# A planned GNN kernel: transfers planned by their size with late landings, PSUM banks held whole in the plan, one bank for each graph at the end, and the weight product cut where the loads of w_ih are cut

## The chip, the core and the metric

The kernel runs on one core of a Trainium2 chip. The metric is the device time of one execution in microseconds. The profile names the engines PE (matrix multiply), PEld (its weight loads), DVE (vector), ACT (scalar, activations), POOL (GpSimd) and SP, whose queue issues all DMAs here. Data is worked on in SBUF; matrix products land in PSUM, which has eight banks of 128 partitions x 512 fp32 columns.

## The reference

128 graphs of 128 nodes with 256 features each. Two blocks, each with a layer norm, a ReLU and a residual sum.

```python
def _L0_gnn_ref(x, adj, weight, w_ih, w_hh, b_ih, b_hh):
    A = (adj != 0).astype(x.dtype)
    h = x
    for i in range(3):
        m = jnp.einsum('bnd,de->bne', h, weight[i])
        aggr = jnp.einsum('bst,bsd->btd', A, m)
        h = _gru_cell(aggr, h, w_ih, w_hh, b_ih, b_hh)
    return h

def _L1_gnn_ref(h, adj, W):
    Wh = jnp.einsum('bnf,fo->bno', h, W)
    s = Wh.sum(axis=-1)
    e = jax.nn.leaky_relu(s[:, :, None] + s[:, None, :], negative_slope=ALPHA)
    e = jnp.where(adj == 0, -jnp.inf, e)
    alpha = jax.nn.softmax(e, axis=-1)
    return jnp.einsum('bpq,bqo->bpo', alpha, Wh)

h = jnp.maximum(_layernorm(x, axis=-1), 0.0)
x = x + _L0_gnn_ref(h, adj, L0_gnn_weight, L0_gnn_w_ih, L0_gnn_w_hh, L0_gnn_b_ih, L0_gnn_b_hh)
h = jnp.maximum(_layernorm(x, axis=-1), 0.0)
x = x + _L1_gnn_ref(h, adj, L1_gnn_W)
```

The GRU cell takes the products `inp @ w_ih.T` and `h @ w_hh.T` (three gates of 256 each), two sigmoids and one tanh.

## The kernel before

**Tiling.** Graphs are taken in 32 groups of four (`G = 4`). A group passes three GRU layers and then the attention. The message weight of a layer is multiplied into `w_ih` once at the start (`compose`, L622), so that a layer needs the edge sums of `h` and then products with two weight sets, `s_hh` (from `w_hh`) and `s_x0`, `s_x1`, `s_x2` (composed). Each product of two 256 x 256 blocks uses seven block products instead of eight: `node_sums` (L850) makes the sums `hs` and `gs` of blocks of data, `block_sums` (L534) those of the weights. Layers 0 and 1 keep features on the partitions (`product`, L887), layer 2 keeps nodes on the partitions (`product_rows`, L901). Several groups are in flight at a time; the list `turns` (L1091) fixes the order of their layers on PE.

**The planner.** Nothing in the loop over groups (L1429) emits an instruction. Each call of `op` (L94) records a node: engine, assumed duration in ns, a function that emits the instructions, and the tiles it reads and writes, from which the dependencies follow. `Plan.run` then orders the nodes and emits them, engine by engine, in that order. Each engine executes its own list in order; an instruction that has to wait holds back all that stand behind it on its engine. The order comes from a list schedule in assumed time (`go`, L247) that is tried many times with shaken priorities (`search`, L212), and the try with the least PE idle time plus a share of a measure of risk is kept. In the first 20 us and the last 120 us of PE work `EDGES` tries are made for each piece of the order, elsewhere `TRIES`.

**What the plan takes a DMA for.** An SP node costs its issue time (`kb * KB` ns in `load`, L500, 480 ns for the later loads) and then a fixed `lag` of 3600 ns (other numbers are given at single calls) until its data is there. If another DMA landed just before, it is taken to land at least `BEHIND` = 1200 ns after that one, whatever its size (L324). `x1` (L1131) and the rows of a later group (L1112) are 512 KB each and are often issued one right after the other. The first reader of the rows is DVE, `bn_stats` (L686) in `normed`.

**What the plan takes a PSUM bank for.** The program itself keeps two engines out of one bank: a bank is one tile. The plan before knows that a new user of a bank waits for the old one, but within one use it compares column ranges: where PE writes half 1 and DVE reads half 0, it takes both to run at the same time.

**The start.** `weights` (L553) loads the weights (two loads for the halves of `w_ih`, L571), transposes them through PSUM (`turned`, L511), composes and makes the block sums. The composed weight of 768 columns is made for each k in pieces of 512 and 256 columns (L619); both halves of `w_ih` must have been transposed for any piece. PSUM tiles are copied out by `to_sbuf` (L529).

**The end.** The third last group's and the second last group's attention ends with a product for each graph (L1286) and an addition into `x1` (L1295); two graphs share a bank, in its two halves. The last group works graph by graph: `weighed` (L1368) turns two graphs in one bank `p_h` (L1379), copies them out (L1382), multiplies them into one bank `p_w` (L1388) and copies that out (L1391); `by_graph` (L1395) has one bank `p_e` for the turned weights (L1404, copied out at L1406) and one bank `p_o` for the products (L1408), which L1411 adds into `x1`; L1414 writes each graph to DRAM. The scores are made in bank `x_n` (L1187, L1193, L1226), the maximum at L1235, the bound `low` at L1230 to L1233, the exponentials at L1250.

## Time and profile before

| what | us |
|---|---|
| median of three runs (2084.32 to 2087.18) | 2086.25 |
| the profiled execution, its own time | 2087.59 |
| its span in the profile | 2085.5 |
| DVE, ACT, POOL busy (share of the span) | 1688.3 (81%), 1619.1 (78%), 910.0 (44%) |

The profiled execution took 2.1 us more than its span, which is what lies before the first and after the last recorded instruction. The granted PE clock is 0.9 or more of full speed in all forty slices of the page. The span less PE's busy time is 16.3 us, and it lies like this:

| stretch of the span (us) | PE idle (us) |
|---|---|
| 0 to 30 | 4.10 |
| 30 to 200 | 0.59 |
| 200 to 1800 | 3.08 |
| 1800 to 2060 | 0.46 |
| 2060 to 2080 | 3.94 |
| 2080 to 2085.5 | 4.10 |

Issued DMAs of 512 KB landed after a median of 5.1 us (rows of a group) and 4.3 us (`x1`), those of 256 KB after 2.8 us, the transposing ones after 3.2 to 3.3 us. A duration of a matmul in the profile holds some 0.16 us in which the next one already runs: two fp32 passes with 256 columns take 0.59 us when they stand alone in a row, and the next row starts 0.43 us after them.

### The profile page before, as it was taken

To read this page: it belongs to the slowest core of one execution; us is meant where nothing else is said; L and a number is where in the kernel's file an instruction comes from. 1 tells how busy PE (TensorE), PEld (TensorE's weight loads), DVE (VectorE), ACT (ScalarE), POOL (GpSimd) and SP (SyncE) were. 2 spreads that over 40 slices of the span, in tenths; PEclk is the share of its full clock that TensorE was granted. 3 is DMA by queue.
4 is the path that set the end of the run, shared out by engine and by line. 5 is a ranking of instruction groups with operands and counts; after the bars stand their busy time and mean duration, and the time that the engine had idled before them with its cause. 6 is when DMAs were issued, how large, how long until landed. Compare 5 with 4: busy or idle time off the path is not lost.

```text
span 2085.5 us, 31660 instructions
## 1 busy us (share of the span) xinstructions
PE 2069.2 (99%) x10926; PEld 1660.3 (80%) x10926; DVE 1688.3 (81%) x3912; ACT 1619.1 (78%) x3007; POOL 910.0 (44%) x885
## 2 busy tenths in 40 slices
PE   9999999999999999999999999999999999999998
PEld 7887887778877778877788877788777888788875
DVE  6777887888878888887888887888888877788677
ACT  6677887788877788877888777878777886878775
POOL 4644544435434435444354434454443544445330
PEclk9999999999999999999999999999999999999999
DMA  5322233332333323233222333232333223323321
GB/s 147 66 64 43 56 69 72 73 69 43 69 74 71 76 47 71 61 79 73 65 49 66 82 66 76 49 64 66 76 76 61 46 67 77 61 44 67 64 66 36
DMA packets 369376, 138.12 MB, mean 66 GB/s; under 512 B 300608, under 2 KB 368960, under 8 KB 369216
## 3 DMA queue, kind: packets, MB, share of 16 engines
q1 hardware_dynamic: 369216, 136.10, 29.6%
q8 instruction: 86, 1.41, 0.3%
q14 instruction: 74, 0.61, 0.1%
HBM read 45.36 MB, written 16.78 MB: 30 GB/s over the span
## 4 chain that ended last, share of the span: by engine, by line
PE 94%; DMA 2%; ACT 1%; DVE 1%; POOL 1%; SPq 0%; issue 0%; ACTq 0%; DVEq 0%; POOLq 0%
PE y_rz L887 15%; PE q_rz L887 10%; PE x_rz L887 10%; PE y_n L887 7%; PE misc L807 6%; PE y_n L901 6%; PE y_rz L901 6%; PE q_n L887 5%; PE x_n L887 5%; PE misc L1326 4%; PE x_n L901 4%; PE q_n L901 4%; PE x_rz L901 4%; PE q_rz L901 4%; PE misc L840 3%; DMA rows<-in_x_dram 2%
## 5 line engine op out<-in xcount | busy, mean ns | idle before, releaser
L856 POOL TENSOR_TENSOR hs<-hT 128x512 f32<-128x512 f32 x96 | 123.0, 1282 | 466.4 <-PE y_n L901 244.9
L764 POOL TENSOR_TENSOR r<-rows 128x512 f32<-128x512 f32 x126 | 137.7, 1111 | 173.0 <-ACT rows L702 91.0
L887 PE MATMUL y_rz<-hs,s_hh 128*128 128x256 f32 x768 | 197.7, 380 | 3.6 <-ACT t_rz L933 3.6
L887 PE MATMUL y_rz<-gs,s_x 128*128 128x256 f32 x768 | 197.2, 379 | 0.0
L943 DVE TENSOR_TENSOR t_rz<-t_rz,q_rz 128x512 f32<-128x512 f32 x192 | 131.4, 684 | 77.2 <-ACT t_rz L933 55.6
L933 ACT COPY t_rz<-y_rz 128x512 f32<-128x512 f32 x192 | 112.0, 583 | 99.9 <-PE y_rz L901 60.7
L887 PEld LDWEIGHTS y_rz<-hs,s_hh 128*128 128x128 f32 x768 | 145.3, 190 | 25.4 <-POOL rs L695 2.8
L860 POOL TENSOR_TENSOR hs<-hT,hs 128x256 f32<-128x256 f32 x96 | 77.6, 809 | 198.2 <-PE q_n L901 160.1
L887 PEld LDWEIGHTS y_rz<-gs,s_x 128*128 128x128 f32 x768 | 145.9, 190 | 19.6
L767 POOL TENSOR_TENSOR p<-r 128x512 bf16<-128x512 f32 x126 | 155.1, 1248 | 2.7
L943 DVE TENSOR_TENSOR t_n<-t_n,q_n 128x512 f32<-128x512 f32 x192 | 131.1, 683 | 29.5 <-PE q_n L901 17.1
L1081 POOL TENSOR_TENSOR x<-x,u 128x512 f32<-128x512 f32 x60 | 78.8, 1315 | 139.6 <-ACT u L1061 139.6
L887 PE MATMUL x_rz<-aT,s_x 128*128 128x256 f32 x512 | 131.5, 379 | 0.0
L887 PE MATMUL x_rz<-hT,s_hh 128*128 128x256 f32 x512 | 131.4, 379 | 0.0
L1017 ACT ACTIVATE u<-u,bias_i 128x512 f32<-128x512 f32 x128 | 91.1, 723 | 36.3 <-DVE u L1008 36.3
L887 PE MATMUL y_n<-hs,s_hh 128*128 128x256 f32 x384 | 114.4, 380 | 0.0
L887 PE MATMUL y_n<-gs,s_x 128*128 128x256 f32 x384 | 114.2, 379 | 0.0
L856 DVE TENSOR_TENSOR gs<-aT 128x512 f32<-128x512 f32 x96 | 91.0, 948 | 27.9 <-ACT aT L813 27.8
L887 PEld LDWEIGHTS x_rz<-hT,s_hh 128*128 128x128 f32 x512 | 97.2, 190 | 19.1
L1338 DVE SCALAR_TENSOR_TENSOR x<-misc,rden,x 128x128 f32<-128x128 f32 x312 | 89.6, 344 | 27.9 <-ACT rz L1043 15.0
L887 PEld LDWEIGHTS x_rz<-aT,s_x 128*128 128x128 f32 x512 | 97.1, 190 | 13.0
L789 POOL TENSOR_TENSOR pl<-d,pl 128x512 bf16<-128x512 f32 x64 | 83.5, 1313 | 50.9 <-ACT pl L787 50.7
(296 smaller groups left out, 6390.4 us busy)
## 6 DMA issues: line engine op xcount, KB each, us to landing
rows<-in_x_dram SPq DMA_DIRECT2D x32, 512.0 KB, 5.1
x<-in_x_dram SPq DMA_DIRECT2D x32, 512.0 KB, 4.3
out_dram<-x SPq DMA_DIRECT2D x31, 512.0 KB, 2.9
at<-in_adj_dram SPq DMA_DIRECT2D x32, 256.0 KB, 2.8
plT<-pl SPq DMA_TRANSPOSE x190, 3.3
peT<-pe SPq DMA_TRANSPOSE x60, 3.2
e<-in_L_gnn_weight_dram SPq DMA_DIRECT2D x3, 256.0 KB, 4.2
rz<-in_L_gnn_w_ih_dram SPq DMA_DIRECT2D x2, 384.0 KB, 4.2
```

The costliest lines, as they stand in the source:

```text
L764: op("POOL", 1042, lambda part=part: nc.gpsimd.tensor_tensor(ap(r1)[:, part], ap(rows)[:, part], top(rows)[:, part], OP.subtract), [(rows, ...
L767: op("POOL", 1042, lambda part=part: nc.gpsimd.tensor_tensor(ap(p3)[:, part], ap(r1)[:, part], top(r1)[:, part], OP.subtract), [(r1, n, n ...
L789: op("POOL", 1158, lambda k=k, r=r: nc.gpsimd.tensor_tensor(part(pl, k, 2), ap(r), part(pl, k, 1), OP.subtract), [r], [(pl, k, k + 1)])
L807: nc.tensor.matmul(flat(pair[k])[:, b * N:(b + 1) * N], part(i, b, k), ap(a)[:, b, :], start=(b == 0 and i == 0), stop=(i == 2), skip_grou ...
L856: op(eng, cost, lambda: sub(ap(w)[:, 0:2, :], blocks()[:, 1::2, :], blocks()[:, 0:2, :], OP.subtract), [t], [(w, 0, 2)], two=True)
L887: nc.tensor.matmul(ap(bank)[:, half, :], ap(w)[:, i - 1, gate, :], source(i, t, sums), start=(first and c == 0 and m == 0), stop=False, sk ...
L901: op("PE", 645, lambda c=c, w=w, t=t, sums=sums: nc.tensor.matmul(flat(bank)[:, c * P:(c + 3) * P], source(i, t, sums)[:, m * N:(m + 1) * ...
L933: op("ACT", 590, lambda: nc.scalar.copy(ap(t), ap(y)), [y], [t], mark=mark)
L943: op("DVE", 690, lambda: nc.vector.tensor_tensor(ap(t), ap(t), ap(q), OP.add), [q], [t])
L1017: op("ACT", 723, lambda j=j, cols=cols: nc.scalar.activation(ap(u)[:, cols], ap(u)[:, cols], AF.Tanh, bias=ap(W["bias_i"])[:, 2 * KD + j:2 ...
L1326: nc.tensor.matmul(ap(b)[:, h, m * P:(m + 1) * P], source(i, uT, sums)[:, m * N:(m + 1) * N], ap(W["w1"])[:, c], start=(first and m == 0), ...
L1338: op("DVE", 340, lambda i=i, m=m: nc.vector.scalar_tensor_tensor(ap(x1)[:, i, j * P:(j + 1) * P], ap(b)[:, h, m * P:(m + 1) * P], ap(rden) ...
```

## The change

- **Transfers by size.** A DMA lands no sooner than `takes` after the one before it; `load` and the later loads give `kb * SERVICE` with 2.85 ns for each KB, so 1459 ns for 512 KB. Lags are set anew.
- **Late landings.** A node may have a `spare`, which readers of it are kept away for in addition: 3400 ns for `x1` and the rows, 2500 ns for the adjacency, 400 ns for the transposing DMAs.
- **Banks held whole.** Each node knows the banks it touches; where it or the other user writes, it starts in the plan only when the last other engine's use is over.
- **A bank for each graph at the end.** In the attention of the last three groups graph b of a pair has bank `ps[b]` for both pairs, `weighed` and `by_graph` use one bank for each graph for all four steps, the first of the two passes' banks being `y_rz` and `x_rz`, those of the second `misc`.
- **Compose split.** Pieces of 384 and 384 columns, each of which waits only for its own half of `w_ih`.
- `EDGES` goes from 60 to 400.

```diff
-TRIES, EDGES, WIDTHS, SHARES = 20, 60, (500, 1500, 4000), (0.1, 0.3, 1.0)
+TRIES, EDGES, WIDTHS, SHARES = 20, 400, (500, 1500, 4000), (0.1, 0.3, 1.0)
...
+SERVICE = 2.85
+X_SPARE, AT_SPARE, T_SPARE = 3400, 2500, 400
...
+    def halves(self, items, is_write):
+        return [(id(x[0]), is_write) for x in items if isinstance(x, tuple) and x[0].tag in self.whole]
...
+    def wait(self, i, u):
+        return self.twait(i, u) + self.nodes[i][10]
...
                     t = max(c + (self.FLIP if s.thin and e == "PE" and not n[8] else 0), at[i])
+                    for b, w in n[11]:
+                        for other, q, free in s.bank.get(b, ()):
+                            if (w or q) and other != e:
+                                t = max(t, free + self.SIGNAL[e])
...
-                late = max(s.landed + self.BEHIND - done - n[7], 0)
+                late = max(s.landed + n[9] - done - n[7], 0)
...
-    def load(dst, get, src, kb, behind=(), lag=3300):
-        op("SP", kb * KB, lambda: nc.sync.dma_start(get(dst), src), behind, [dst], lag=lag)
+    def load(dst, get, src, kb, behind=(), lag=2300):
+        op("SP", kb * KB, lambda: nc.sync.dma_start(get(dst), src), behind, [dst],
+           lag=lag, takes=kb * SERVICE)
...
-                for g0, gn in ((0, 512), (512, 3 * D - 512)):
+                for g0, gn in ((0, 3 * P), (3 * P, 3 * P)):
...
-                       [(wT, half * GN, (half + 1) * GN)] + w_ihT, [ps])
+                       [(wT, half * GN, (half + 1) * GN)] + [(b, g0, g0 + gn) for b in w_ihT], [ps])
...
-                load(t, ap, src, kb, lag=4800 if t is at else 3300)
+                load(t, ap, src, kb, lag=2300 if t is at else 3500)
             else:
-                op("SP", 480, lambda t=t, src=src: nc.sync.dma_start(ap(t), src), [], [t])
+                op("SP", 480, lambda t=t, src=src: nc.sync.dma_start(ap(t), src), [], [t],
+                   lag=2400 if t is at else 3600, takes=kb * SERVICE, spare=AT_SPARE if t is at else X_SPARE)
...
+        two_banks = ([late_bank(t) if g == NG - 2 else buf("misc") for t in ("q_rz", "q_n")]
+                     if g >= NG - 3 else ())
         for m in range(lo, hi, 2) if g >= SEVEN else ():
-            ps = late_bank(("q_rz", "q_n")[m // 2]) if g == NG - 2 else buf("misc")
+            ps = two_banks or [buf("misc")] * 2
...
-        p_h, p_w = (late_bank(t) for t in (("y_rz", "y_n") if lo else ("x_rz", "y_n")))
+        ps = [buf("misc"), buf("misc")] if lo == 0 else [late_bank("y_rz"), late_bank("x_rz")]
...
-                    nc.tensor.transpose(ap(p_h)[:, b - lo, k * P:(k + 1) * P],
+                    nc.tensor.transpose(ap(ps[i])[:, 0, k * P:(k + 1) * P],
...
-                    nc.tensor.matmul(ap(p_w)[:, i, :], ap(hT)[:, k, i * N:(i + 1) * N],
+                    nc.tensor.matmul(ap(ps[i])[:, 1, :], ap(hT)[:, k, i * N:(i + 1) * N],
...
-        p_e, p_o = (late_bank(t) for t in (("q_rz", "q_n") if lo else ("y_rz", "x_rz")))
+        rows_w, ps = rows_w
...
-                ap(p_e)[:, i, :N], ap(e)[:, b, :], ident), [(e, b, b + 1)], [(p_e, i, i + 1)])
+                ap(ps[i])[:, 0, :N], ap(e)[:, b, :], ident), [(e, b, b + 1)], [(ps[i], 0, 1)])
...
-                ap(p_o)[:, i, :], ap(eT)[:, b, :], ap(rows_w)[:, i * D:(i + 1) * D], start=True, stop=True),
+                ap(ps[i])[:, 1, :], ap(eT)[:, b, :], ap(rows_w)[:, i * D:(i + 1) * D], start=True, stop=True),
```

## The prediction

> **What bounds the kernel now.** I read the page's first part, then who waited for whom on PE, then the same for DVE. The columns of the waits are total us, times, longest.
>
> ```profile
> PE 2069.2 (99%) x10926; PEld 1660.3 (80%) x10926; DVE 1688.3 (81%) x3912; ACT 1619.1 (78%) x3007; POOL 910.0 (44%) x885
> ```
>
> ```profile
> PE y_rz L887 <- ACT t_rz L933: 3.6, 6, 0.9
> ```
>
> ```profile
> DVE st L686 <- DMA rows<-in_x_dram: 37.1, 25, 3.6
> ```
>
> PE is busy for 99% of the span. The change keeps PE's work (the two compiled programs differ by one matmul instruction in 6632), so it can only take from the 16.3 us of idle time, and from a drain of about 0.16 us behind each stall (0.59 us for a pair of 256-column passes against 0.43 to the next start), which counts as busy. The question is which stalls go. The second fence names the largest kind: PE waits for ACT's copy of `y_rz`, six times. The third holds the root, on another engine: of 28 groups whose rows arrive during the run, 25 or so make DVE stand still for them. Followed back, the longest of the six is this piece of the chain of waits (start, duration, what):
>
> ```profile
> 1358.57 0.58 SPq L1131
> 1359.15 0.34 issue
> 1359.49 5.33 DMA rows<-in_x_dram
> 1364.82 0.02 issue
> 1364.84 1.41 DVE st L686 x4
> 1366.25 0.28 DVE mv L691 x4
> 1366.53 0.69 DVE low L1245
> 1367.21 0.02 issue
> 1367.24 1.28 ACT e L1250 x4
> 1368.52 0.36 ACT rz L993
> 1368.88 0.36 ACT rz L1011
> 1369.23 0.48 ACT t_rz L933
> ```
>
> SP issues `x1` (L1131) and then the rows (L1112), 512 KB each. The rows land after 5.33 us; the plan took 3.6. DVE stands at `bn_stats`, and behind it in DVE's list is `low` of another group, which does not need the rows. ACT stands at the exponentials that need `low`, and behind them is the copy that PE needs. The same chain, always with `x1` just ahead of the rows, reaches PE at 349, 541, 605, 987 and 1370 us: 3.0 us of idle time (3.6 less 0.6 for the sixth, at 143.6 us, which hangs on a transposing DMA of 3.81 us).
>
> At the end I read DVE's and ACT's timelines (start, duration, engine, operation):
>
> ```profile
> 2058.90 0.48 DVE L1295 SCALAR_TENSOR_TENSOR x<-misc,rden,x 128x256 f32<-128x256 f32 x1 [0.99 <-PE misc L1286]
> 2059.30 0.15 DVE L1230 TENSOR_TENSOR top<-top,s 128x4 f32<-128x4 f32 x1
> ```
>
> ```profile
> 2059.95 0.40 ACT L1250 ACTIVATE s_all<-s_all,low 128x128 f32<-128x128 f32 x1 [1.58 <-DVE low L1233]
> ```
>
> The first product is read only when the second graph's product, in the same bank, is done; the bound `low` stands behind that read and ACT idles 1.58 us.
>
> **The change part by part.** I take positions from the compiled order of the changed program and durations from this trace; line numbers are those of before.
>
> *Late landings and sizes.* They add no instruction. 18 loads of `x` still stand directly ahead of another in SP's list (24 before), so transfers are hardly faster; what moves is the reader. In DVE's list of before the first `bn_stats` of a new group stands 26 instructions after the last addition into `x1` of the attention, in most groups; now mostly 30 to 41. Eight instructions of some 0.43 us (1688 us over 3912) are 3.4 us, against a longest wait of 3.6. Is there room behind? In the group above `bn_stats` end at 1366.5, the reciprocal roots on POOL take 1.3 us, yet `nm` (L698) runs at 1374.1 and ACT's `h` (L702) at 1374.9: over 5 us of slack, so the rows' later reading costs nothing. If that cover were gone, PE would wait for the group's first product. Here a rule speaks against the change: the Trainium skill, "DMA: Bandwidth & Descriptors", section "Anatomy of one DMA — SWDGE (gpsimd) path", has a fixed 2.0 us plus bytes over 436 GB/s, fitted for GpSimd's DMAs. An estimate by it for 512 KB is 3.2 us, the old 3.6 would be enough, the spare would gain nothing. The trace has 5.1 us (median) and 5.33 here, behind another 512 KB; I take the trace. Gain: 3.0 + 5 x 0.16 = **3.8 us**. Bounds: 2 (some stay) to 4.
>
> *Other small stalls in the middle* (143.6: 0.6; near 1799: 0.4; near 2012: 0.1, plus drains 0.5) come from chains of three engines; a new order draws them anew. Bounds: loses 1 to gains 1.5. I take **0.2**.
>
> *The start.* In PE's list the first pieces of compose (384 columns, four passes of 0.323 us each from L901's pairs, 1.29 us) now stand after the first transposes of the second half of `w_ih`. The wait for that half (0.61 us at 6.83) stays. The next waits of before, 0.61 for the second message weight and 0.24 for `uT`, get 2.6 us of compose ahead of them. But the copy of the second piece stands on DVE behind three `bn_stats` of the first rows, which land at 9.62: 9.65 + 3 x 0.33 + 0.56 = 11.2, so PE's second message transpose waits from 10.36: 0.9. Issue for issue PE is 0.4 us ahead at 14.05. Then DVE decides. These are its rows:
>
> ```profile
> 14.61 1.36 DVE L548 TENSOR_TENSOR s_x<-h 128x384 f32<-128x384 f32 x1
> ...
> 19.43 0.53 DVE L546 TENSOR_TENSOR s_x<-s_x,h 128x384 f32<-128x384 f32 x1
> ```
>
> One operation takes 1.36 us while POOL runs `s_hh` sums (14.43 to 15.54) and 0.53 alone. The Trainium skill, "SBUF — State Buffer", section "SBUF: two separate sides", says that DVE with two SBUF inputs and GpSimd share a port pair as an exclusive lock and the loser blocks. In the new list three such sums (L544, L546, L548) stand ahead of the copies that free the banks for the rows' transposes, and POOL's sums start at the same copy of `u`. All alone they would be 1.6 us and PE's stall there some 0.8; with two of them at 1.3 they are 3.1, the bank comes free at 20.05 and PE waits from 17.96: 2.1, against 1.4 issue for issue before (16.2 to 17.6). I take the contended row: 0.4 - 0.7 = **-0.3**. Bounds: -1.2 to +1.
>
> *The end.* Walked through the lists, in the clock of before:
> 1. L1187 (0.43) moves ahead of the products of the third last group, which now end at 2060.86. `low` no longer stands behind their reads: L1217 2055.9, t2 sum, maximum 2057.1 to 2057.7, L1065, three small ones: exponentials at 2058.5 instead of 2059.95. PE is late next: transposes (L1268) at 2060.86 instead of 2061.66.
> 2. Copy 0.59, two products and copies as before: products of the second last group start at 2064.66 (2065.39), and L1187 is gone from among them: end 2068.11 (2069.38).
> 3. `nm` and the last tanh no longer stand behind a late q product on DVE: `h` at 2067.0 (2067.81). Its transposes follow at 2068.11. Four copies of 0.37 and four half-bank products of 0.86 a graph now overlap in two banks: end 2070.65 (2072.44).
> 4. The score sums L1193 come after them, so leaky runs at 2071.3 (2070.55) and the first exponential at 2073.05 (2073.01): nothing gained for the first pair.
> 5. The second pair: `nm` at 2072.3 (2073.62), `h` 2072.45 (2074.05), score sums ahead of the products: `low` 2075.7 (2078.46), exponentials 2076.05 (2078.95).
> 6. Then turn, copy (0.29), product 0.43 and addition per graph: the last addition ends at 2079.4 (2082.67). Behind it the store, as before (landing 1.8 us).
>
> **3.3 us**. Bounds: 1.3, if step 4's delay carries to the end; 4.0.
>
> *Banks held whole* adds no wait in the program, which had them already; `EDGES` only chooses. Both are in the lists read above.
>
> Sum: 3.8 + 0.2 - 0.3 + 3.3 = 7.0. The profiled execution of before took 2087.59 with 2.1 us around its span: 2080.6 of that kind. It was 1.3 above the median shown, 2086.25, so against the median **2079.3 us**.
>
> **Rivals.** 0.2% is 4.2 us, what a measurement of this kernel tells from no change.
>
> - *The forecast*, mid-run and end both gain: own range 2076.5 to 2082, chance 0.66.
> - *Only one part pays.* The end is bound by DVE, which has few gaps from 2055 to 2069, and step 4 shows that the score sums can eat a gain; then 1.3 + 3.8 + 0.2 - 1.2 = 4.1 at worst, or 3.7 with no gain at the end at all. Against: three separate waits go there. 2082.5, chance 0.19.
> - *It does not do what it says*: landings are late by more than 7 us (one, of all the rows, took 9.4), or as many new stalls appear as go: 2086, chance 0.08.
> - *Slower: the spare is paid on PE.* The rows' chain (statistics, roots, ReLU, split, transposes, `hs`) starts 3.4 us later in each of some 25 groups. If a group's slack is under 3.4 us, PE waits 0.4 + 0.16 per group: 14 us, less the 7.0 of the sum: 2093. From seven such waits (3.9 us) the gain of the middle is gone, from 13 (7.3 us) the sign turns. Against it is the slack of over 5 us; for it that I read it in one group. Chance 0.07.
>
> **The numbers.** The likeliest case gives 2079.3. The range 2075.8 to 2084.5 takes in the bounds of the start and the end and nearly all of the second case; outside are most of the last two. Faster by over 0.2% (below 2082.1): 0.66 and half of the second case, rounded to 0.75. Within 0.2%: the rest of it and the third, 0.17. Slower: the fourth and a bad draw, 0.08.
>
> **What would show it.** DVE's wait for rows falls from 37.1 us to under 5 with 5 us landings unchanged; PE's wait `y_rz` on `t_rz` goes from six times to one or none; the idle time from 200 to 1800 us drops from 3.1 to under 1. DVE's wait at L1295 for the `misc` product is no longer in front of `low`, and from the start of the products L1286 of the third last group to the end of the span it takes 24.8 us instead of 28.5. In the first 20 us PE waits about as long as before, once for a copy of a bank behind contended sums. It would be wrong if PE shows new waits for `hs` or `hT` in the middle, or if the exponentials of the last pair still run 6.5 us before the end.

## The result, and the profile after

| | median (us) | runs, lowest to highest | profiled execution | its span |
|---|---|---|---|---|
| before | 2086.24 | 4: 2084.32 to 2087.18 | 2087.59 | 2085.5 |
| changed | 2077.00 | 4: 2076.00 to 2077.78 | 2076.59 | 2074.8 |

The ratio is 0.9954, with a 95% interval of 0.9942 to 0.9966. By the medians the change gains 9.2 us, by the spans 10.7: the profiled execution of before took 1.35 us more than its median, that of the changed kernel 0.41 less. So some 1.5 us of what the stretches below gain lies between these two executions, and can't be placed. The lines of the code have moved down by 16 to 25: L686 is now L704, L887 is L905, L933 is L951, L1286 is L1308, L1295 is L1319, L1326 is L1350.

The first part of the page of the changed kernel, engine by engine (busy time, share of the span, instructions):

```profile
PE 2065.2 (100%) x10926; PEld 1660.6 (80%) x10926; DVE 1700.0 (82%) x3912; ACT 1625.8 (78%) x3007; POOL 920.1 (44%) x885
```

The count of instructions is the same on every engine. PE's idle time went from 16.3 us to 9.6, and its busy time fell by 4.0 with the same 10926 matmuls: this second part is time that sits in the durations of the matmuls ahead of a wait. By the starts of PE's passes some 2.7 us of it are the drains behind stalls that are gone (27 gaps in PE's work before, 12 after), and 1.2 us are waits too short to show as idle time. DVE and ACT are busy for 11.7 and 6.7 us longer, in a shorter span: they are not what bounds it.

The waits of DVE, then of PE, in the changed kernel (total us, times, longest):

```profile
DVE st L704 <- DMA rows<-in_x_dram: 0.5, 1, 0.5
```

```profile
PE y_rz L497 <- DVE zeros L494: 1.2, 1, 1.2
PE x_n L1207 <- DVE top L1255: 1.2, 1, 1.2
PE misc L631 <- DVE hT L549: 0.9, 1, 0.9
PE q_n L1308 <- ACT uT L865: 0.7, 1, 0.7
PE x_rz L858 <- ACT eT L1290: 0.7, 1, 0.7
PE misc L735 <- DVE h L549: 0.6, 1, 0.6
PE misc L541 <- DMA rz<-in_L_gnn_w_ih_dram: 0.4, 1, 0.4
PE y_rz L1413 <- ACT uT L1407: 0.2, 1, 0.2
```

DVE stood still for rows 25 times and 37.1 us; now once. The six waits of `y_rz` on `t_rz` have gone. What is left on PE belongs to the first 20 us (L497, L541, L631, L735) and the last 25 (L858, L1207, L1308, L1413). The rows still take a median of 5.0 us to land (5.1 before), so transfers are not faster; readers come later. The stretch in the middle, as a view by stretch shows it for the changed kernel (busy us and instructions of PE, PE's loads, DVE, ACT, POOL; granted clock; DMA share; GB/s):

```profile
200.00:1800.00 1600.00, 1600.00 (x8567) 1292.40 (x8566) 1342.57 (x3105) 1279.79 (x2348) 724.51 (x684) 1.00 0.30 67
```

No idle time is left on PE in 1600 us, where 3.08 us were. To count the hidden waits too, I take PE's passes in a stretch by form, give each the interval at which such passes follow each other undisturbed (0.216 us for 256 fp32 columns, 0.323 for 384, 0.429 for 512, 0.108 for 128, 0.056 for 128 in bf16), and subtract the sum from the stretch. The remainder, called *loss* below, is not nought even where PE is never idle (8.7 us in the middle of the changed kernel), so only its differences count. For the end I take the time from where the last pass of the GRU's products has started and PE is free for the next row (2056.98 before, 2049.03 after) to the end of the span.

| stretch (us) | before: idle, loss | after: idle, loss | gained |
|---|---|---|---|
| 0 to 30 | 4.09, 5.3 | 3.30, 4.3 | 1.0 |
| 30 to 200 | 0.59, 1.2 | 0, 0.3 | 0.9 |
| 200 to 1800 | 3.08, 14.1 | 0, 8.7 | 5.4 |
| 1800 to 2040 | 0.46, 1.8 | 0.10, 1.0 | 0.8 |
| the end, as defined | 28.5 long | 25.8 long | 2.7 |

Up to rounding these are the 10.7 us of the spans. Late landings and the small stalls were priced at 4.0 and brought 7.0 (the three middle rows); the end was priced at 3.3 and brought 2.7; the start was priced at a loss of 0.3 and gained 1.0.

### The profile page after: what moved, and what is told of

The parts are those of the page before. It is cut to its first block, busy times and chain, and to the rows that moved or that the text cites. A ratio compares the mean times of both kernels' runs of the same rounds, so it can differ in the third digit from the quotient of the medians.

```text
span 2074.8 us, 31658 instructions
## 1 busy us (share of the span) xinstructions
PE 2065.2 (100%) x10926; PEld 1660.6 (80%) x10926; DVE 1700.0 (82%) x3912; ACT 1625.8 (78%) x3007; POOL 920.1 (44%) x885
## 3 DMA queue, kind: packets, MB, share of 16 engines
q1 hardware_dynamic: 369216, 136.10, 29.6%
## 4 chain that ended last, share of the span: by engine, by line
PE 99%; ACT 0%; DMA 0%; DVE 0%; SPq 0%; issue 0%
PE y_rz L905 16%; PE q_rz L905 11%; PE x_rz L905 11%; PE y_n L905 8%; PE misc L825 6%; PE y_n L919 6%; PE y_rz L919 6%; PE x_n L905 5%; PE q_n L905 5%; PE x_n L919 4%; PE misc L1350 4%; PE q_n L919 4%; PE x_rz L919 4%; PE q_rz L919 4%; PE misc L858 3%; PE misc L1308 1%
## 5 line engine op out<-in xcount | busy, mean ns | idle before, releaser
L782 POOL TENSOR_TENSOR r<-rows 128x512 f32<-128x512 f32 x126 | 155.2, 1244 | 186.4 <-ACT rows L720 65.7
L905 PE MATMUL y_rz<-hs,s_hh 128*128 128x256 f32 x768 | 197.3, 379 | 0.0
L905 PE MATMUL y_rz<-gs,s_x 128*128 128x256 f32 x768 | 197.1, 379 | 0.0
L951 ACT COPY t_rz<-y_rz 128x512 f32<-128x512 f32 x192 | 112.5, 586 | 94.2 <-PE y_rz L919 51.0
L905 PEld LDWEIGHTS y_rz<-gs,s_x 128*128 128x128 f32 x768 | 145.9, 190 | 19.8
L905 PEld LDWEIGHTS y_rz<-hs,s_hh 128*128 128x128 f32 x768 | 144.3, 190 | 19.0 <-POOL p L785 0.3
L785 POOL TENSOR_TENSOR p<-r 128x512 bf16<-128x512 f32 x126 | 148.6, 1190 | 4.3
L905 PE MATMUL x_rz<-hT,s_hh 128*128 128x256 f32 x512 | 131.5, 379 | 0.0
L905 PE MATMUL x_rz<-aT,s_x 128*128 128x256 f32 x512 | 131.4, 379 | 0.0
L874 DVE TENSOR_TENSOR gs<-aT 128x512 f32<-128x512 f32 x96 | 85.6, 892 | 37.5 <-ACT aT L831 37.1
L905 PE MATMUL y_n<-hs,s_hh 128*128 128x256 f32 x384 | 114.3, 379 | 0.0
L905 PE MATMUL y_n<-gs,s_x 128*128 128x256 f32 x384 | 114.2, 379 | 0.0
L905 PEld LDWEIGHTS x_rz<-hT,s_hh 128*128 128x128 f32 x512 | 97.1, 190 | 19.3
L905 PEld LDWEIGHTS x_rz<-aT,s_x 128*128 128x128 f32 x512 | 97.1, 190 | 13.1
L1038 DVE TENSOR_TENSOR d<-hT,u 128x512 f32<-128x512 f32 x128 | 100.2, 787 | 7.9 <-ACT u L1035 7.7
L831 ACT COPY aT<-misc 128x512 f32<-128x512 f32 x190 | 101.1, 584 | 4.6 <-PE misc L825 4.4
```

Source lines behind the costliest of these rows:

```text
L782: op("POOL", 1042, lambda part=part: nc.gpsimd.tensor_tensor(ap(r1)[:, part], ap(rows)[:, part], top(rows)[:, part], OP.subtract), [(rows, ...
L785: op("POOL", 1042, lambda part=part: nc.gpsimd.tensor_tensor(ap(p3)[:, part], ap(r1)[:, part], top(r1)[:, part], OP.subtract), [(r1, n, n ...
L831: op("ACT", 590, lambda k=k: nc.scalar.copy(ap(dst)[:, k, :], flat(pair[k])), pair[k:k + 1], [(dst, 2 * k, 2 * k + 2)])
L874: op(eng, cost, lambda: sub(ap(w)[:, 0:2, :], blocks()[:, 1::2, :], blocks()[:, 0:2, :], OP.subtract), [t], [(w, 0, 2)], two=True)
L905: nc.tensor.matmul(ap(bank)[:, half, :], ap(w)[:, i - 1, gate, :], source(i, t, sums), start=(first and c == 0 and m == 0), stop=False, sk ...
L951: op("ACT", 590, lambda: nc.scalar.copy(ap(t), ap(y)), [y], [t], mark=mark)
```

## The experiments

Each was run with a profile and timed beside the kernel before. "Loss" and "end" are those of the table above, from the one profiled execution; the ratio is against the kernel before as it ran beside each of them (medians of 2086.21 to 2086.92). Differences of variants among themselves have no interval of their own. The end starts with the last pass of the GRU, and some orders have more of PE's other work ahead of that pass: with equal work the ends of a_seed, no_hold, old_both and end_misc are 25.4, 25.8, 29.6 and 25.8.

| kernel | median (us) | ratio, 95% interval | middle: idle, loss | end (us) | DVE's waits for rows (us, times) |
|---|---|---|---|---|---|
| before | 2086.24 | | 3.08, 14.1 | 28.5 | 37.1, 25 |
| b_seed | 2083.91 | 0.9986 (0.9979 to 0.9992) | 1.00, 10.8 | 27.2 | 28.1, 24 |
| b_spare | 2083.13 | 0.9984 (0.9977 to 0.9991) | 0.07, 10.1 | 27.4 | 0.7, 1 |
| b_hold | 2081.31 | 0.9975 (0.9967 to 0.9983) | 0.37, 9.7 | 24.7 | 34.0, 25 |
| old_both | 2081.07 | 0.9973 (0.9963 to 0.9983) | 0, 9.5 | 30.0 | none |
| no_hold | 2077.74 | 0.9959 (0.9944 to 0.9974) | 0, 9.5 | 25.4 | none |
| no_spare | 2076.17 | 0.9954 (0.9939 to 0.9969) | 0.25, 8.7 | 24.2 | 31.1, 19 |
| old_dma | 2076.26 | 0.9952 (0.9937 to 0.9967) | 0.23, 9.5 | 24.2 | 30.6, 23 |
| end_old | 2075.58 | 0.9948 (0.9933 to 0.9963) | 0, 8.7 | 25.5 | none |
| end_misc | 2076.25 | 0.9955 (0.9940 to 0.9970) | 0, 8.7 | 26.3 | none |
| edges60 | 2077.00 | 0.9956 (0.9941 to 0.9971) | 0, 7.6 | 24.4 | none |
| a_seed | 2079.07 | 0.9966 (0.9953 to 0.9979) | 0.56, 9.2 | 23.7 | none |
| compose_old | 2077.84 | 0.9960 (0.9946 to 0.9975) | 0.12, 8.7 | 25.8 | 1.1, 1 |
| changed | 2077.00 | 0.9954 (0.9942 to 0.9966) | 0, 8.7 | 25.8 | 0.5, 1 |

### Late landings: taken out, and given to the kernel before alone

no_spare, against the changed kernel:

```diff
-X_SPARE, AT_SPARE, T_SPARE = 3400, 2500, 400
+X_SPARE, AT_SPARE, T_SPARE = 0, 0, 0
```

> The changed kernel with all three spares set to 0; sizes, lags, held banks, end and start stay. If the spares took the stalls on late rows away, DVE waits again for rows in 20 or more groups (25 to 37 us in all) and PE for y_rz on t_rz some four to six times; the time goes back by 2 to 4 us, to 2079 to 2081. If planning by sizes alone (1459 ns behind the transfer before) is enough, or if the gain in the middle was a lucky draw of the order, DVE's wait stays under 10 us and the time within 1 us of 2077.

b_spare, against the kernel before (a node gets a `spare`, which `wait` adds):

```diff
-        return 0 if a[0] == b == "PE" else a[7] + self.SIGNAL[b]
+        return (0 if a[0] == b == "PE" else a[7] + self.SIGNAL[b]) + a[9]
...
-                op("SP", 480, lambda t=t, src=src: nc.sync.dma_start(ap(t), src), [], [t])
+                op("SP", 480, lambda t=t, src=src: nc.sync.dma_start(ap(t), src), [], [t], spare=0 if t is at else 3400)
...
-                    ap(x1), x[graphs].rearrange("b n d -> n b d")), [], [x1])
+                    ap(x1), x[graphs].rearrange("b n d -> n b d")), [], [x1], spare=3400)
```

> The kernel before with one part alone: a spare of 3400 ns for the later loads of x, nothing else. If late rows are the cause of the five stalls, DVE's wait for rows falls from 37 us to under 5 and PE's stalls behind it go: 3 to 4.5 us faster than before, 2082 to 2083. If the spare is paid back on PE (the rows' chain starts 3.4 us later in each group), the time is 2086 or more.

old_dma goes one step past no_spare: besides the spares, all lags and the times for the size of a transfer (`takes`) are those of before again. Of the diff:

```diff
-    def load(dst, get, src, kb, behind=(), lag=2300):
+    def load(dst, get, src, kb, behind=(), lag=3300):
...
-            lag=lag, takes=kb * SERVICE)
+            lag=lag)
...
-                load(t, ap, src, kb, lag=2300 if t is at else 3500)
+                load(t, ap, src, kb, lag=4800 if t is at else 3300)
...
-                   lag=2400 if t is at else 3600, takes=kb * SERVICE, spare=AT_SPARE if t is at else X_SPARE)
+                   )
```

> The changed kernel with every assumption on transfers as before: no spares, 1200 ns behind the transfer before whatever its size, the old lags. Without spares the time stayed at 2076.2 although DVE waited 31 us for rows. If planning by sizes was what kept those waits from PE, PE now waits for y_rz behind late rows four times or more and loses 2 to 4 us, 2078.5 to 2081. If late rows only reach PE by the draw of the order, or if held banks and the rest suffice, PE's idle time from 200 to 1800 us stays under 1 us and the time within 1.2 us of 2077.

b_spare behaves as the chain in the prediction says. Its waits of DVE for rows, and PE's for ACT's copy:

```profile
DVE st L686 <- DMA rows<-in_x_dram: 0.7, 1, 0.7
```

```profile
PE y_rz L887 <- ACT t_rz L933: 0.4, 1, 0.4
```

The reader comes later, and one wait of 0.4 us, at 1890 us, is left of six: the middle gains 4.0 us of loss. (Some 1.0 us is given back from 1800 to 2040, in waits of the new order.) This count of waits is what speaks for the chain. The time does not: b_seed, a mere other draw of the order, is as fast as b_spare (see below). The two kernels without spares then say something that I had not expected. The waits for rows in no_spare, and its middle stretch:

```profile
DVE st L704 <- DMA rows<-in_x_dram: 31.1, 19, 4.3
```

```profile
200.00:1800.00 1600.00, 1599.75 (x8566) 1292.56 (x8565) 1347.71 (x3102) 1273.52 (x2347) 729.17 (x685) 1.00 0.30 67
```

DVE again stands still for rows, once for 4.3 us, longer than any wait before, and PE is idle for 0.25 us in 1600. The late rows are back and no longer reach PE. Which link of the chain is gone can be read from ACT's waits for `low`, here of before, b_hold (further down), old_dma and no_spare:

```profile
ACT e L1250 <- DVE low L1245: 31.1, 23, 2.4
```

```profile
ACT e L1261 <- DVE low L1256: 25.3, 19, 4.0
```

```profile
ACT e L1269 <- DVE low L1264: 22.3, 20, 3.1
```

```profile
ACT e L1270 <- DVE low L1265: 9.4, 12, 2.1
```

In before the five longest of these, 2.1 to 2.4 us and each just behind late rows, are followed by PE's five stalls; the other 18 are at most 1.44 us and none is followed by one. In b_seed two of 2.3 us are followed by stalls of 0.5. In b_hold and old_dma ACT waits nearly as long in all, but behind late rows only one wait is over 1.44 us: 1.9 in b_hold, followed by 0.12 us on PE. (Their longest, 4.0 and 3.1, are not behind rows, and PE stands still after neither.) In no_spare `low` itself stands behind the rows less often. In the changed kernel the spares, the lags and the times by size are worth nothing that can be measured: medians of 2076.17 and 2076.26 against 2077.00.

### Banks held whole: taken out, and given to the kernel before alone

no_hold, against the changed kernel (the planner no longer keeps the other engine off a held bank):

```diff
-                            if (w or q) and other != e:
+                            if 0 and (w or q) and other != e:
```

> The changed kernel whose plan no longer waits for another engine's use of the same bank; the program's own waits stay. If knowing the banks removed the short waits within the seven products (in the trace of before the rows of that line take 1.4 us longer in all, over 728 passes) and the odd stalls of the middle that hang on no transfer, then these come back: 1.5 to 3 us slower, 2078.5 to 2080. If those went by the spares or by chance, the time stays within 1 us of 2077.

The middle loses 0.7 us more (9.5 against 8.7), in waits too short to show, and the end is no longer than with the rule. So with spares and own banks in place the rule is worth less than 1 us by the trace, within what another order of the changed kernel does (7.6 in edges60, 9.2 in a_seed); by the medians (2077.74 against 2077.00) nothing can be told.

b_hold, against the kernel before: the planner's rule for held banks and nothing else.

```diff
+    def halves(self, items, is_write):
+        return [(id(x[0]), is_write) for x in items if isinstance(x, tuple) and x[0].tag in self.whole]
...
+                    for b, w in n[9]:
+                        for other, q, free in s.bank.get(b, ()):
+                            if (w or q) and other != e:
+                                t = max(t, free + self.SIGNAL[e])
...
+            for b, w in n[9]:
+                s.bank[b] = [x for x in s.bank.get(b, ()) if x[0] != e or x[1] != w] + [(e, w, done + n[7])]
```

> The kernel before with one part alone: the plan holds banks whole; transfers, end, compose and 60 tries as before. If held banks alone were enough, idle from 200 to 1800 us falls from 3.1 to under 0.7 although DVE still waits 25 us or more for rows, the end takes under 26.5 us instead of 28.5, and the time is 2077 to 2079. If the parts need each other, idle there stays over 1.5 us and the time at 2080 or more.

DVE's waits for rows in b_hold, and PE's longest waits of the same kernel:

```profile
DVE st L697 <- DMA rows<-in_x_dram: 34.0, 25, 3.9
```

```profile
PE y_rz L491 <- DVE zeros L488: 1.2, 1, 1.2
PE misc L837 <- DVE hT L542: 1.2, 1, 1.2
PE x_n L534 <- DMA rz<-in_L_gnn_w_ih_dram: 0.9, 1, 0.9
PE y_rz L898 <- ACT t_rz L944: 0.7, 2, 0.5
```

As many late rows as before, and nearly as long, but the wait on ACT's copy falls from 3.6 us to 0.7 and the loss of the middle from 14.1 to 9.7. So the stalls can go in two ways: by reading the rows later (b_spare, 10.1), or in an order made with the banks known (b_hold, 9.7). Both together give 8.7, not the sum. But the draw alone, in b_seed, has 10.8 with 24 late rows, so for b_hold the rule and its draw are not told apart. The median of b_hold was above what I had expected: the first 30 us lose 6.1 instead of 5.3 (the wait of 1.2 us for `hT` was there before), and from 1800 to 2040 it loses 2.4 instead of 1.8. The latter is of its own order, not of held banks as such: no_spare and old_dma, with the same rule, have 0.9 and 0.7 there.

Held banks also remove short waits that no idle time shows. The groups of the seven-product rows by form (count, busy us, mean ns, then idle time in front), of no_hold and then of the changed kernel, which differ by the rule alone:

```profile
L1350 PE MATMUL misc<-w,h 128*128 128x128 f32 x416 | 63.5, 275 | 0.0
L1350 PE MATMUL misc<-w,uT 128*128 128x128 f32 x312 | 49.6, 282 | 0.0
```

```profile
L1350 PE MATMUL misc<-w,h 128*128 128x128 f32 x416 | 63.1, 275 | 0.0
L1350 PE MATMUL misc<-w,uT 128*128 128x128 f32 x312 | 49.0, 279 | 0.0
```

The same 728 instructions take 113.1 us without the rule and 112.1 with it. The two other pairs that differ by it alone have 113.5 and 112.6 (before, b_hold) and 113.1 and 112.0 (old_both, end_old). Over all fourteen kernels the two sums do not overlap: 113.1 to 113.8 in the five without it (before, b_seed, b_spare, no_hold, old_both), 111.3 to 112.7 in the nine with it. Some 1 us of the rule's gain is thus shown apart from the draw.

### The end: a bank for each graph, or one for two

end_old, against the changed kernel: all of the end's banks are those of before. Of the diff its core:

```diff
-        two_banks = ([late_bank(t) if g == NG - 2 else buf("misc") for t in ("q_rz", "q_n")]
-                     if g >= NG - 3 else ())
...
-            ps = two_banks or [buf("misc")] * 2
+            ps = late_bank(("q_rz", "q_n")[m // 2]) if g == NG - 2 else buf("misc")
...
-        ps = [buf("misc"), buf("misc")] if lo == 0 else [late_bank("y_rz"), late_bank("x_rz")]
+        p_h, p_w = (late_bank(t) for t in (("y_rz", "y_n") if lo else ("x_rz", "y_n")))
...
-        rows_w, ps = rows_w
+        p_e, p_o = (late_bank(t) for t in (("q_rz", "q_n") if lo else ("y_rz", "x_rz")))
```

> The changed kernel with the shared banks of before in the attention of the last three groups. If a bank for each graph brought the gain at the end, the stretch from the end of the last product row to the end of the span goes from 25.8 us back to about 28.5, and the time to 2079 to 2080. If the gain at the end came from the plan (held banks, 400 tries), the stretch stays under 26.5 us and the time within 1 us of 2077.

old_both is end_old with the line of no_hold as well: neither remedy, with all else of the change.

> The changed kernel with the shared banks at the end and without held banks in the plan; 400 tries, spares, sizes and the split compose stay. Each of the two alone left the end at 25.4 us. If either of them is enough, taking both away brings the end back to 27.5 to 28.5 us, and with the short waits of the middle the time is 2079.5 to 2081. If the 400 tries made the end, it stays under 26.5 us and the time at 2077 to 2078.5.

The end is 25.5 us with the old banks and 30.0 without the rule too, and the medians of this pair, 2075.58 and 2081.07, are 5.5 us apart. The waits that came up in old_both:

```profile
PE y_n L858 <- ACT eT L1290: 0.8, 1, 0.8
PE y_rz L1288 <- ACT s_all L1270: 0.7, 1, 0.7
...
PE y_n L1408 <- ACT d L1411: 0.6, 1, 0.6
PE x_rz L1428 <- DVE eT L1426: 0.4, 1, 0.4
```

The first is in every kernel here. L1288 waits for exponentials, as the products before it are done sooner than these; L1408 waits for ACT's copy out of the bank that two graphs share; L1428 for a copy of turned weights, the last of a chain that has come late by then. The changed kernel has none of the last three. Not all of the 30.0 us are such waits: the clock has a part. The rows of one product on PE in old_both and in end_old, and a stretch of old_both around it (the granted clock is the third number from the end):

```profile
2056.84 2.07 PE L858 MATMUL y_n<-eT,h 128*128 128x128 f32 x8 [0.82 <-ACT eT L1290]
```

```profile
2053.14 1.16 PE L858 MATMUL y_n<-eT,h 128*128 128x128 f32 x8 [0.68 <-ACT eT L1290]
```

```profile
2058.00:2060.00 2.00, 2.00 (x12) 2.00 (x11) 2.00 (x6) 0.65 (x2) 0.23 (x1) 0.50 0.03 8
```

From 2056.8 to 2060.2 PE works at half the clock, and the 16 passes of L858 take 3.4 us to the start of the next row where they take 1.9 in end_old: 1.5 us. Six of the nine runs of old_both have a mean clock below 1.000; they took 2080.91 us or more, the other three 2079.66 to 2079.83. So beside the changed kernel some 2.7 us of the 4.1 are left to the two parts together.

Over all kernels, with equal work: with neither remedy the end takes 27.1 to 29.6 us (before, b_seed, b_spare, old_both; 28.1 for the last less its 1.5 us), with at least one 24.2 to 25.8 (the other ten), with own banks alone 25.8 (no_hold), with the rule alone 24.6 to 25.8 (b_hold, end_old, end_misc). The bank for each graph is one way to 2 or 3 us, not the only one, and not needed beside the other.

end_misc is end_old with a bank of its own for the scores of one pair of the last group, against the wait of L1207:

```diff
-            s_all = late_bank("x_n")
+            s_all = late_bank("x_n") if lo else buf("misc")
```

> The version that was fastest so far (shared banks at the end, all else changed: 2075.6) with a bank of its own for the scores of the last pair of graphs (misc instead of x_n). If the wait of PE for DVE's read of the shared score bank (1.2 us in the changed kernel) is on the path of the end, it is 0.5 to 1.2 us faster, 2074.4 to 2075.1. If that wait lies beside the path, the end stays within 0.3 us of 25.4 and the time at 2075.3 to 2076.

The end takes 26.3 us (25.8 with equal work), so nothing is gained. But the run does not answer its question: end_old, which it was made from, has no such wait of PE at L1207 either; of the kernels made from the changed one only compose_old has the 1.2 us too. Whether they cost anything there is open: no_spare, old_dma and edges60, with 0.3 us there, have ends of 24.2 to 24.4 us, no_hold with 0.3 has 25.8.

### The draw of the order

The planner tries orders at random from a fixed seed. b_seed and a_seed change the seed, in the kernel before and in the changed one; edges60 puts back the 60 edges.

```diff
-        dice, nodes = Random(1), self.nodes
+        dice, nodes = Random(2), self.nodes
```

> The kernel before with another seed for the shaken priorities, nothing else. It tells how much is the draw. If the five stalls on late rows follow from the plan's ignorance, four to eight of them appear again at other places, 3 us idle or more from 200 to 1800 us, and the time is 2084.5 to 2088. If they were a bad draw, idle there is under 1.5 us and the time 2082 to 2084.

> The changed kernel with another seed for the shaken priorities, nothing else. If the gain follows from what the plan knows, idle from 200 to 1800 us is again under 0.3 us, the end under 26.5 us and the time 2075.5 to 2078.5. If this order was a lucky draw, some of it goes: 2079 or more.

```diff
-TRIES, EDGES, WIDTHS, SHARES = 20, 400, (500, 1500, 4000), (0.1, 0.3, 1.0)
+TRIES, EDGES, WIDTHS, SHARES = 20, 60, (500, 1500, 4000), (0.1, 0.3, 1.0)
```

> The changed kernel with 60 tries at the edges instead of 400. If the gain at the end came from the larger search, the stretch from the last product row to the end of the span goes from 25.8 us to 27 or more and the time to 2078.5 or more. If it came from held banks or from the banks for each graph, either of which was enough alone, the stretch stays under 26.5 us and the time within 1 us of 2077.

By the medians the other seed makes the kernel before 2.3 us faster (2.9 by the ratio) and the changed one 2.1 us slower (2.5). In a_seed PE waits for ACT's copy again:

```profile
PE y_rz L905 <- ACT t_rz L951: 1.3, 2, 0.9
```

In b_seed that wait is 1.2 us, three times, where the kernel before has 3.6, six times, with 24 late rows against 25: how many late rows reach PE is a matter of the draw as well. Its gain is larger than its median says. In its trace PE waits 2.2 us for the second half of `w_ih`, and from 8 to 16 us the granted clock is 0.50 to 0.72; so only the middle and the end of this trace are read here. Of its 20 runs 13 have a mean clock below 1.000, with a median of 2084.62 us; the seven at 1.000 have 2081.28, some 5 us below the kernel before and what b_hold has (2081.31). In the other twelve traces the clock is full wherever PE works. Just before the drop PE had little to do in both: no pass for 2.2 us here, four passes in 3.1 us in old_both; two cases, no more. edges60 has the same median as the changed kernel: a new stall between 1800 and 2040 us, `q_rz` on `gs` for 1.5 us, and an end of 24.4 us instead of 25.8 set each other off. So one draw was worth 2 to 3 us in the changed kernel and up to 5 in the kernel before, and a difference of that size between two kernels of this table is not put down to their edit by its median alone. The counts of stalls, and sums over many kernels, carry more.

### Compose split

compose_old, against the changed kernel:

```diff
-                for g0, gn in ((0, 3 * P), (3 * P, 3 * P)):
+                for g0, gn in ((0, 512), (512, 3 * D - 512)):
...
-                       [(wT, half * GN, (half + 1) * GN)] + [(b, g0, g0 + gn) for b in w_ihT], [ps])
+                       [(wT, half * GN, (half + 1) * GN)] + w_ihT, [ps])
```

> The changed kernel with compose in pieces of 512 and 256 columns that wait for both halves of w_ih. If the split brought the 1.1 us that the first 30 us of the run lost less, these come back: what PE loses there goes from 4.1 us to 5 or more, 2078. If the start came from the plan's better loads and copies, it stays under 4.5 us and the time within 0.8 us of 2077.

The first 30 us lose 4.1 us with the old pieces and 4.3 with the new: the split is not what gained at the start, and no gain by it is seen anywhere.

## Why the prediction was right or wrong

**The sum (7.0 us).** 9.2 us were measured by the medians, inside the range. The total held because it was read from the compiled order of the changed program, and that holds whatever has put an operation where it stands. What was read from it is which waits would go; the credit to single parts was argued, and most of it did not hold: each of the parts, taken out alone, leaves a median of 2075.58 to 2077.84 us. That the errors of the terms stay inside the range is in part luck: by the spans, start and small stalls were put too low by 1.3 and 3.0 us, the end too high by 0.6.

**Late landings and sizes (3.8 us).** Right in the chain: with the spare alone, in b_spare, the rows' waits go, PE's waits go with them, and the middle gains 4.0 us. Wrong in what the changed kernel owes to it. The chain has three links, and only the first was looked at: the rows are late, `low` stands behind them on DVE, the exponentials and the copy stand behind `low` on ACT. In the three kernels with held banks and without spares the first link stays (31 us of waiting in no_spare) and hardly any stall on PE follows: the long waits of ACT behind late rows are gone. The estimate of 3.2 us for 512 KB, by the fixed cost of the Trainium skill ("DMA: Bandwidth & Descriptors", section "Anatomy of one DMA — SWDGE (gpsimd) path"), is too low beside the 5.0 us measured; yet what I concluded from the trace against it, that the spare is needed, did not hold in the changed kernel, for another reason.

**Other small stalls (0.2 us).** Mis-sized. The three middle stretches gained 7.0 us, less the 3.8 of the rows: 3.2. By the starts of PE's passes about half of it, 1.5, is the three stalls named, of which the new order drew hardly one anew (0.1 us idle are left from 30 to 2040 us), and 1.6 are waits that do not show as idle time, of which the seven-product rows alone have 1.4 (113.5 to 112.1 us). I had bounded the term by 1.5, because I counted only waits that show.

**The start (-0.3 us).** Wrong in one term, the sums beside POOL. These are DVE's rows and then POOL's of the changed kernel (start, duration, what):

```profile
15.61 0.55 DVE L562 TENSOR_TENSOR s_x<-h,hT 128x384 f32<-128x384 f32 x1
...
16.41 1.02 DVE L564 TENSOR_TENSOR s_x<-s_x,h 128x384 f32<-128x384 f32 x1
17.36 0.55 DVE L566 TENSOR_TENSOR s_x<-h 128x384 f32<-128x384 f32 x1
```

```profile
15.77 1.25 POOL L566 TENSOR_TENSOR s_hh<-u 128x384 f32<-128x384 f32 x1 [2.68 <-DVE u L549]
17.56 1.20 POOL L562 TENSOR_TENSOR s_hh<-u,u 128x384 f32<-128x384 f32 x1 [0.54 <-ACT u L549]
```

I took two sums at 1.3 us, 3.1 with the third; they took 2.1, since only one of the three began while a sum of POOL ran. The stall behind them, and the one that I had put at 0.9 us:

```profile
11.15 0.44 PE L631 MATMUL misc<-ident,e 128*128 128x128 f32 x2 [0.87 <-DVE hT L549]
18.75 0.66 PE L735 MATMUL misc<-ident,rows 128*128 128x128 f32 x4 [0.63 <-DVE h L549]
```

The 0.9 is right (0.87). The stall at the bank, put at 2.1, is 0.63. With 1.5 us less there the term becomes 1.2, and 1.0 was measured.

**The end (3.3 us).** Right within 0.6 us in size, by the steps of the walk. Shifted so that the products of the third last group start together, the walk had the exponentials 1.1 us behind that start, the second last group's products at 7.25, the transposes at 10.7, the end of the first pair's products at 13.24 and the last addition's end at 22.0. The rows of DVE, ACT and PE in the changed kernel, where the first of these products start at 2049.45:

```profile
2050.31 0.17 DVE L1253 TENSOR_SCALAR low<-top 128x4 f32<-128x4 f32 x1
...
2064.44 0.42 DVE L1255 TENSOR_REDUCE top<-x_n 128x2 f32<-128x256 f32 x1 [1.90 <-ACT s_all L1246]
2064.78 0.15 DVE L716 SCALAR_TENSOR_TENSOR nm<-mv,rs 128x2 f32<-128x2 f32 x1
...
2071.06 0.92 DVE L1436 SCALAR_TENSOR_TENSOR x<-misc,rden,x 128x256 f32<-128x256 f32 x2
```

```profile
2050.57 0.40 ACT L1270 ACTIVATE s_all<-s_all,low 128x128 f32<-128x128 f32 x1 [0.34 <-DVE low L1253]
...
2068.54 0.42 ACT L1270 ACTIVATE s_all<-s_all,low 128x128 f32<-128x128 f32 x1
```

```profile
2049.45 3.62 PE L1308 MATMUL misc<-w,uT 128*128 128x256 f32 x16
...
2056.91 1.13 PE L1308 MATMUL q_n<-w,uT 128*128 128x256 f32 x4 [0.68 <-ACT uT L865]
...
2060.47 0.38 PE L1404 MATMUL y_rz<-ident,h 128*128 128x128 f32 x2
...
2063.14 0.61 PE L1213 MATMUL x_n<-ident,s 128*128 128x128 f32 x4
```

They are at 1.1, 7.46, 11.0, 13.69 and 22.5. `low` no longer stands behind a read of L1319, and ACT's idle time ahead of the exponentials is 0.34 us instead of 1.58. The half microsecond was lost in steps 2 and 3 (0.45 by the end of the first pair's products), and the later steps carry it. What was wrong is the reason. The walk put the gain of the order that it read down to the bank for each graph; end_old has the old banks and an end of 25.5 us, no longer than the 25.8 of the changed kernel.

**Banks held whole (nothing).** This is the term that was wrong in its reason. "Adds no wait in the program, which had them already" is true, but a gain does not follow only from waits added or removed: the planner had taken two engines to share a bank at one time, so part of the plan's overlap could not happen. Taken as it is in the changed program, the rule was "in the lists read", and so its gain was counted there under other names. What it is worth: about 1 us in the seven-product rows, in three pairs; and at the end, where banks are shared, it is one of two ways to some 2 or 3 us. Given to the kernel before alone, it has 0.9975 (0.9967 to 0.9983), some 5.2 us, where the spare alone has 0.9984 (0.9977 to 0.9991), some 3.3 us. But b_seed, with nothing but another draw, has 0.9986 (0.9979 to 0.9992), and with the clock at full as little time as b_hold. So neither number is shown to be the part's own.

**Compose, `EDGES`.** No gain was priced for either and none was found.

**The rivals.** The slower case, a spare paid on PE, did not come: PE is idle for 0.1 us in all between 30 and 2040 us, so no group's slack was too small. "Only one part pays" fell too, since both stretches gained. "It does not do what it says" holds for the spares in one sense: they do move the readers, and the kernel is as fast without them.

**The signs.** DVE's and PE's waits and the idle time of the middle came out as named. From the start of the third last group's products to the end of the span 24.8 us were named; 25.4 were measured, and 28.5 before. One sign for being wrong could tell nothing: the exponentials of the last pair start 6.3 us before the end (2068.54), in the walk itself 6.2, and before 6.6.

**What stays open.** In no_spare, old_dma and b_hold, made with the banks held, late rows cost PE next to nothing; before and in b_seed they cost it five stalls and two. Whether that is the rule or the draw of three orders is not shown. Nor is it told apart how much of the last 2 to 3 us between variants is the draw: each plan was run with two seeds at most. The fastest kernel run is end_old, 2075.58 us (0.9948, 0.9933 to 0.9963), with held banks and shared ones at the end; its lead of 1.4 us over the changed kernel is less than a draw is worth.

## What to carry to other kernels

Where a planner makes the order, make its model wait for what the program waits for (here a whole bank) before adding margins. Two remedies for the same stall do not add, so take a part out of the new kernel *and* put it alone into the old one before giving it credit. A late transfer costs the bounding engine only through the in-order queues between them, so count the stalls that arrive, not those at the transfer. Run the same planner with other seeds, the old kernel's too, to learn what a draw is worth, and look at the granted clock before putting a difference down to waits.

## What the runs showed of the hardware

A sum of two SBUF operands on DVE (128x384, fp32) that begins while such a sum runs on POOL waits for POOL's to end: L564 begins at 16.41, POOL's ends at 17.02, and 0.41 us later the sum is done, 1.02 in all against 0.55. Before, L548 began at 14.61 and POOL's ended at 15.55: 0.41 later it was done, 1.36 in all. The fourteen traces have 26 such cases, and in each DVE's sum ends 0.41 to 0.42 us after POOL's. It holds the other way round: where POOL's sum begins 0.1 to 0.7 us after DVE's, DVE's is not held up by it (0.55 us in the changed kernel), and POOL's ends 0.86 to 0.87 us after DVE's. `bn_stats` (L704 at 16.07, 0.42 us) takes no longer beside POOL than elsewhere. All this fits the rule of an exclusive lock with a loser that blocks, which the prediction cited from the Trainium skill, "SBUF — State Buffer", section "SBUF: two separate sides". The same section says that the one that starts first has the ports for its whole instruction. That is what I left out: the order of the starts decides which of the two loses.
